# A 1x1 convolution to 128 channels as four tiles of 32 columns: one edit in a block-matching and convolution kernel

## The chip, the cores and the metric

The kernel runs on one core of a Trainium2 chip. The metric is the device time of one execution in microseconds (us). A core has five engines that run their own instruction streams in order and wait for each other by semaphores: TensorE (PE in the profile, with its weight loads under PEld), VectorE (DVE), ScalarE (ACT), GpSimd (POOL) and SyncE (SP). In this kernel the last two mostly issue DMAs.

## The reference

The input `x` is f32, 8 images of 32 channels of 128x128. Layer 0 normalises the image by groups of two channels and finds, for each pixel, the 8 of 25 shifts of the image whose 3x3 patches are nearest. It gathers the 8 shifted copies (32 x 8 = 256 channels), runs them through three pairs of a 1x1 convolution over all 256 channels and a 3x3 convolution of each channel by itself, and uses the result as a weight on a small transform of the gathered channels. Layer 1 is a 5x5 convolution of each channel. Cut to what matters:

```python
xb = _patch_match_stack(x)                                   # [8, 256, 128, 128]
dct = _conv(xb, dct_w, groups=C)
h = relu(_conv(_conv(xb, w1), w2, groups=CK, pad=1))         # w1, w3, w5: 256 x 256, 1x1
h = relu(_conv(_conv(h, w3), w4, groups=CK, pad=1))          # w2, w4, w6: 3x3 by channel
wiener = sigmoid(_conv(_conv(h, w5), w6, groups=CK, pad=1))
filt = _conv(wiener * dct, inv_dct_w, groups=C)
return _conv(filt, agg_w)
```

The change is in the 1x1 convolutions with w1, w3 and w5. All arithmetic in question is f32.

## The kernel before

An image is cut into 16 blocks of 8 rows (`R = 8`, `NS = 16`), with a 17th step that finishes the last rows. `steps` lists the 8 x 17 = 136 pairs of image and block. The main loop runs over the steps, and in each it works on four stages, `for i in (3, 2, 1, 0)`: the third, second and first pair of convolutions, each for a step that lies further back, and the end of layer 0. The instruction order of TensorE, VectorE and ScalarE is the order of the calls in this loop, written out by hand (`manual_schedule(engines=ORDERED)`). The order of the DMAs on POOL and SP is left to the scheduler.

The 256 channels are two halves of 128. Of each half a 1x1 convolution needs all 256 input channels, so two accumulating products (`g` in 0, 1) with 128 input channels each. The two halves of the output are treated differently:

- VectorE's half, output channels 128 to 255. `pointwise_v` (lines 639 to 657) computes the 1x1 convolution with channels on the partitions: for each tile of four rows (`h` in 0, 4) it takes a PSUM tile `ps` (named `pv...`) of 128 partitions x 512, and line 649 puts in the products of the weights `lhsT[:, g, P:CK]` (128 x 128) with four rows of 128 pixels. ScalarE copies the tile into `tv` (line 657). `depthwise_v` then does the 3x3 convolution: the first tap on ScalarE (line 700) and eight taps on VectorE (line 703), then the activation function (line 707).
- TensorE's half, output channels 0 to 127. `pointwise_t` (lines 659 to 687) writes 32 output channels and one of four rows into each quarter of the partitions, by products of 32 columns (line 673, tile `p...`), ScalarE copies them into `t` (line 680), and SP shifts rows between partitions by DMA (lines 685 and 687). `depthwise_t` does the 3x3 convolution by products of 32 columns with a banded matrix (line 729, tile `pw...`). ScalarE applies the activation (line 742).

Beside these, TensorE's stream holds the gather of the shifted copies (`gather_pixels`, line 611, tile `pg...`, 88 products of 32 columns at a time as the profile counts them), sums for the block matching (line 436, `pd`, 32 columns), the small transform and the end of layer 0 (line 788, `pc`, 64 columns; line 809, `pa`, 32 columns), transposes (lines 390, 502 and 546, 128 columns) and the 5x5 convolution of the image before (line 902, 64 columns).

Around a call of `pointwise_v` the order on TensorE is: `pointwise_v` of the stage; what other queues hold (`run("P")`, `final_dct`, `run("Q")`); `pointwise_t` of the same stage; `gather_pixels`; `depthwise_t` of the stage before. A product of f32 operands is two instructions with a weight load each in the profile, so a call of `pointwise_v` for a whole block (2 tiles x 2 halves) shows as 8 products.

The PSUM tiles of all these stages but `pw` and `pd` come from one pool, `ps_x`, with five buffers in turn.

Of the kernel before, what the change touches and what calls it, by code (L numbers as in the profile page):

```python
# [15 lines left out]
P = 128  # L16
C, K, H, W = 32, 8, 128, 128
CK = C * K
# [24 lines left out]
def bm3d_conv_preact(  # L43
# [16 lines left out]
    nc = tc.nc  # L60
# [578 lines left out]
    def pointwise_v(i, b, n, lhsT, src):  # L639

        v = tv[i - 1]
        if n == NS:
            nc.gpsimd.memset(v[:, i + 1 : 6], 0.0)
        r0, r1 = (i - 1 if n == 0 else 0), (R if n < NS else i - 1)
        for h in range(0, r1, 4):
            hr = min(4, r1 - h)
            ps = ps_x.tile([P, 4, W], F32, name=f"pv{i}_{b}_{n}_{h}", tag="x")
            for g in range(2):
                nc.tensor.matmul(  # L649
                    ps[:, :hr],  # L650
                    lhsT[:, g, P:CK],
                    src(g)[:, h : h + hr],
                    start=g == 0,
                    stop=g == 1,
                )
            a = max(h, r0)
            nc.scalar.copy(v[:, 2 + a : 2 + h + hr, 1 : 1 + W], ps[:, a - h : hr])  # L657

# [324 lines left out]
    def source(i, b, n):  # L983
        src = xbs.pop((b, n), None) if i == 1 else accs.pop((i - 1, b, n))
        return (lambda g: src[:, g]) if i == 1 else (lambda g: src[g])
# [27 lines left out]
    with tc.manual_schedule(engines=ORDERED):  # L1013
# [19 lines left out]
        for s in range(len(steps) + 2):  # L1033
# [10 lines left out]
            for i in (3, 2, 1, 0):  # L1044
# [6 lines left out]
                if live and i:  # L1051
                    src = source(i, bi, ni)
                    pointwise_v(i, bi, ni, lws[i - 1], src)
                    new_v, new_t = depthwise_v(i, bi, ni), depthwise_t(i, bi, ni)
                    accs[i, bi, ni] = [None, next(new_v)]
# [100 lines left out]
```

## Time and profile before

| | us |
|---|---|
| median of 3 runs | 6806.48 (6804.09 to 6808.73) |
| profiled execution, span | 6807.3 |
| TensorE busy, all | 6354.3 |
| of it products at line 649 (pv) | 980.7 + 477.4 |
| products at line 729 (pw) | 2144.1 |
| products at line 673 (p) | 989.1 + 468.1 |
| products at line 611 (pg) | 592.7 |
| VectorE busy, all | 5860.4 |
| of it line 703 (3x3 taps) | 4032.9 |
| ScalarE busy, all | 5064.6 |

The span is the time from the first to the last instruction of one profiled execution. Busy time is the time in which at least one instruction of an engine or group was under way; the products of a group overlap, so a busy time is less than the count times the mean. A form such as `128*32 128x512` is a product whose weights have 128 rows and 32 columns, with 512 streamed elements on each partition. The rows of the costliest groups that belong to the changed function and to its nearest kin (line, engine, operation, tiles, form, count, busy us, mean ns, idle before):

```profile
L673 PE MATMUL p<-acc,lw 128*32 128x256 f32 x16768 | 989.1, 381 | 25.3 <-ACT tv L657 22.7
L649 PE MATMUL pv<-acc,lw 128*128 128x512 f32 (+1 forms) x2112 | 980.7, 607 | 29.9 <-DVE acc L796 27.4
...
L657 ACT COPY tv<-pv 128x512 f32<-128x512 f32 (+2 forms) x784 | 438.1, 578 | 390.4 <-PE pv L649 374.2
```

Products into `p` and `pv` from `acc` handle as many channels and pixels: 16768 products of 32 columns and 256 elements are busy for 989.1 us, 2112 of 128 columns and 512 elements for 980.7 us. The same two stages have further groups that read `xb` in place of `acc`.

### The profile page before, as it was taken

How to read it: one execution, taken by the hardware profiler on the slowest of the kernel's cores; microseconds unless marked ns; L12 is line 12 of the kernel's file. 1: busy time of each engine (PE TensorE's matmuls, PEld its weight loads, DVE VectorE, ACT ScalarE, POOL GpSimd, SP SyncE). 2: the span in 40 equal slices, each digit the busy share in tenths (PEclk: the TensorE clock that was granted, in tenths of full speed). 3: DMA queues.
4: the chain of work that ended last, by engine and by line, in shares of the span. 5: the costliest groups of instructions: out<-in, count | busy, mean ns of one | idle time of the engine just before them, and what ended most of it. 6: DMA issues, size and time to landing. Idle time of an engine off the chain costs nothing.

```text
span 6807.3 us, 257036 instructions
## 1 busy us (share of the span) xinstructions
PE 6354.3 (93%) x113378; PEld 3352.8 (49%) x113378; DVE 5860.4 (86%) x8822; ACT 5064.6 (74%) x6698; POOL 3246.7 (48%) x5351
## 2 busy tenths in 40 slices
PE   5798899999999999999999999999999999999997
PEld 1454454554545455454554455545555454455553
DVE  7789988989889898898988888899888899877776
ACT  5787778777687777877777777877769777687772
POOL 7354446444464444544445444454436554344334
PEclk8899999999999999999999999999999999999998
DMA  4566656666566675666756656566665666566653
GB/s 90 143 153 153 151 149 154 159 152 158 147 156 155 144 169 135 163 151 152 167 135 158 161 146 169 138 165 159 149 150 151 162 156 152 138 170 157 154 151 80
DMA packets 809627, 1021.41 MB, mean 150 GB/s; under 512 B 255456, under 2 KB 619936, under 8 KB 808512
## 3 DMA queue, kind: packets, MB, share of 16 engines
q0 software_dynamic: 422432, 745.61, 42.9%
q1 hardware_dynamic: 383568, 258.11, 17.4%
q8 instruction: 892, 14.61, 0.9%
q10 hardware_dynamic: 2512, 1.25, 0.1%
q14 instruction: 223, 1.83, 0.1%
HBM read 553.25 MB, written 217.01 MB: 113 GB/s over the span
## 4 chain that ended last, share of the span: by engine, by line
PE 55%; DVE 23%; ACT 8%; DMA 6%; issue 5%; POOL 3%; SPq 0%; ACTq 0%; DVEq 0%; POOLq 0%
PE pw L729 18%; DVE acc L703 15%; PE pv L649 13%; PE p L673 12%; PE pg L611 4%; DVE df L421 3%; PE pc L788 2%; DMA t<-t 2%; PE p L902 2%; ACT df L429 2%; ACT ib L596 2%; DVE idx L514 1%; PE pa L809 1%; DMA xf<-xbd 1%; DVE acc L796 1%
## 5 line engine op out<-in xcount | busy, mean ns | idle before, releaser
L703 DVE SCALAR_TENSOR_TENSOR acc<-tv,dwv,acc 128x1024 f32<-128x1024 f32 (+3 forms) x3264 | 4032.9, 1237 | 249.6 <-ACT acc L700 140.3
L729 PE MATMUL pw<-t,dwd 96*32 96x254 f32 (+7 forms) x31680 | 2144.1, 422 | 84.7 <-issue 40.5
L729 PEld LDWEIGHTS pw<-t,dwd 96*32 96x32 f32 (+1 forms) x31680 | 1103.9, 111 | 906.6 <-issue 440.7
L582 POOL DMA_DIRECT2D ib<-idxd x1024 | 570.7, 558 | 1796.5 <-ACT sel L597 1620.6
L596 ACT ACTIVATE ib<-ib,nplace 128x1024 bf16<-128x1024 bf16 x1024 | 1170.1, 1143 | 9.5 <-DMA ib<-idxd 9.5
L597 ACT ACTIVATE sel<-ib 128x1024 f32<-128x1024 bf16 x1024 | 1084.8, 1059 | 32.5
L673 PE MATMUL p<-acc,lw 128*32 128x256 f32 x16768 | 989.1, 381 | 25.3 <-ACT tv L657 22.7
L649 PE MATMUL pv<-acc,lw 128*128 128x512 f32 (+1 forms) x2112 | 980.7, 607 | 29.9 <-DVE acc L796 27.4
L769 POOL DMA_DIRECT2D xf<-xbd x1088 | 650.2, 630 | 304.2 <-PE pc L788 87.0
L673 PEld LDWEIGHTS p<-acc,lw 128*32 128x32 f32 x16768 | 556.2, 111 | 454.9 <-ACT tv L657 62.5
L657 ACT COPY tv<-pv 128x512 f32<-128x512 f32 (+2 forms) x784 | 438.1, 578 | 390.4 <-PE pv L649 374.2
L611 PEld LDWEIGHTS pg<-sel,xt 128*32 128x32 f32 x45056 | 575.5, 111 | 252.1 <-issue 54.2
L429 ACT ACTIVATE df<-df 128x786 f32<-128x786 f32 (+2 forms) x576 | 468.0, 859 | 291.9 <-DVE df L421 289.2
L611 PE MATMUL pg<-sel,xt 128*32 128x48 f32 x45056 | 592.7, 207 | 80.4 <-ACT sel L597 46.0
L421 DVE TENSOR_TENSOR df<-xn 128x786 f32<-128x786 f32 (+2 forms) x576 | 532.5, 976 | 116.0 <-PE pd L436 109.2
L742 ACT ACTIVATE acc<-pw 128x512 f32<-128x512 f32 (+2 forms) x808 | 439.9, 573 | 249.7 <-PE pw L729 249.0
L649 PEld LDWEIGHTS pv<-acc,lw 128*128 128x128 f32 x2112 | 384.2, 193 | 475.6 <-issue 398.1
L707 ACT ACTIVATE acc<-acc 128x1024 f32<-128x1024 f32 (+3 forms) x408 | 416.8, 1022 | 229.7 <-DVE acc L703 229.5
L680 ACT COPY t<-p 128x512 f32<-128x512 f32 x800 | 424.6, 570 | 127.7 <-PE p L673 125.7
L700 ACT ACTIVATE acc<-tv,dwv 128x1024 f32<-128x1024 f32 (+3 forms) x408 | 454.5, 1114 | 52.6 <-PE pa L809 35.0
L649 PE MATMUL pv<-xb,lw 128*128 128x512 f32 x1024 | 477.4, 609 | 0.0
L673 PE MATMUL p<-xb,lw 128*32 128x256 f32 x8192 | 468.1, 380 | 4.4 <-DVE xy L914 4.4
(151 smaller groups left out, 5782.5 us busy)
## 6 DMA issues: line engine op xcount, KB each, us to landing
ib<-idxd POOLq DMA_DIRECT2D x1024, 256.0 KB, 4.4
xbd<-xb POOLq DMA_DIRECT2D x128, 1024.0 KB, 6.7
xf<-xbd POOLq DMA_DIRECT2D x960, 128.0 KB, 7.3
t<-t SPq DMA_DIRECT2D x792, 128.0 KB
t<-t SPq DMA_DIRECT2D x384, 256.0 KB
tv<-tv SPq DMA_DIRECT2D x384, 130.0 KB
xt<-xtd POOLq DMA_DIRECT2D x240, 176.0 KB, 4.6
xl<-xs POOLq DMA_DIRECT2D x256, 64.0 KB, 2.6
```

Of the source, the lines that this page charges most:

```text
L421: nc.vector.tensor_sub(df[:, :, ca:cz], xn[:, r0 : r0 + SR, ca:cz], xn[:, r0 + dy : r0 + dy + SR, ca + dx : cz + dx],)
L429: nc.scalar.activation(df[:, :, ca:cz], df[:, :, ca:cz], AF.Square)
L582: nc.gpsimd.dma_start(ib.rearrange("p k y x -> p (k y x)"), idxd[b][s4 // 8, s4 % 8, 4 * k0 : 4 * k0 + 8] .rearrange("k x -> (k x)") .part ...
L596: nc.scalar.activation(ib, ib, AF.Square, bias=nplace)
L597: nc.scalar.activation(sel, ib, AF.Relu, scale=-1.0, bias=1.0)
L611: nc.tensor.matmul(pg[C * j : C * (j + 1), :, xa:xz], xt[:, t], sels[j // 2][:, j % 2, :, xa:xz], start=True, stop=True,)
L649: nc.tensor.matmul(ps[:, :hr], lhsT[:, g, P:CK], src(g)[:, h : h + hr], start=g == 0, stop=g == 1,)
L673: nc.tensor.matmul(ps[C * r : C * (r + 1), e, :nb], lhsT[:, g, s], rows[:, r : r + 4 * nb - 3 : 4], start=g == 0, stop=g == 1,)
L700: nc.scalar.activation(acc, rows, AF.Copy, scale=tap)
L703: nc.vector.scalar_tensor_tensor(acc, rows, tap, acc, op0=ALU.mult, op1=ALU.add)
L729: nc.tensor.matmul(pt[u][C * j : C * (j + 1), ka:kz, :nb, xa:xz], dwd[0:hi, i - 1, u, j, dx + 1], t[0:hi, j, ka:kz, :nb, xa + dx : xz + dx ...
L769: nc.gpsimd.dma_start(xf[p : p + C, m, j0:j1], src[g, m, (h + m + 1) % 2, :, :, ya:yz])
```

## The change

In `pointwise_v` each product of 128 output columns becomes four products of 32 columns, `j` in 0 to 3. Product `j` takes the columns `P + 32 j` to `P + 32 (j + 1)` of the weights and writes the partitions `32 j` to `32 (j + 1)` of the same PSUM tile. All four stream the same rows. The loop over `g` stays outside, so each quarter still accumulates over the two halves of the input channels.

```diff
             for g in range(2):
-                nc.tensor.matmul(
-                    ps[:, :hr],
-                    lhsT[:, g, P:CK],
-                    src(g)[:, h : h + hr],
-                    start=g == 0,
-                    stop=g == 1,
-                )
+                for j in range(4):
+                    nc.tensor.matmul(
+                        ps[C * j : C * (j + 1), :hr],
+                        lhsT[:, g, P + C * j : P + C * (j + 1)],
+                        src(g)[:, h : h + hr],
+                        start=g == 0,
+                        stop=g == 1,
+                    )
             a = max(h, r0)
             nc.scalar.copy(v[:, 2 + a : 2 + h + hr, 1 : 1 + W], ps[:, a - h : hr])
```

The order of instructions on VectorE and ScalarE is the same in both programs, and so is that on TensorE apart from these products. Some DMA issues on POOL and SP stand in a slightly different order.

## The prediction

> **What bounds the kernel now.** I read the page's busy shares first, then the busy time by stretches, then the chain of waits, then the timeline of TensorE's weight loads, and last the list of TensorE's waits.
>
> ```profile
> PE 6354.3 (93%) x113378; PEld 3352.8 (49%) x113378; DVE 5860.4 (86%) x8822; ACT 5064.6 (74%) x6698; POOL 3246.7 (48%) x5351
> ...
> q8 instruction: 892, 14.61, 0.9%
> ...
> PE 55%; DVE 23%; ACT 8%; DMA 6%; issue 5%; POOL 3%; SPq 0%; ACTq 0%; DVEq 0%; POOLq 0%
> ```
>
> TensorE is busy for 93% of the span, VectorE for 86%. The chain that ended last runs over TensorE for 55% and over VectorE for 23%, so a saving on TensorE counts only in part. Busy time by stretches, first of everything, then of what touches pv, tells how much idle there is after the start-up (columns: microseconds, then busy time and instructions by engine, then granted clock, DMA share, GB/s):
>
> ```profile
> 270.00:6740.00 6470.00, 6178.01 (x111288) 3277.62 (x111287) 5632.97 (x8166) 4910.98 (x6484) 3044.41 (x5068) 0.98 0.62 152
> ...
> sum 6808.00, PE 1458.12 PEld 569.75 ACT 438.15; mean PE 486.04 PEld 189.92 ACT 146.05
> ```
>
> From 270 to 6740 us TensorE is idle for 6470.0 - 6178.0 = 292 us, 4.5%. The products into pv, which the change rewrites, keep it busy for 1458 us. The chain of the whole span gives L649 13.3%, 0.133 x 6807.3 = 905 us: 905 / 1458 = 62% of pv lies on the path that sets the end. A stretch of that chain, in order of time (start, length, what):
>
> ```profile
> 3023.29 0.80 PE pd L436 x8
> 3024.09 3.45 PE p L673 x64
> 3027.54 0.91 PE pg L611 x88
> 3028.45 3.63 PE pv L649 x8
> 3032.08 3.59 PE p L673 x64
> 3035.67 0.91 PE pg L611 x88
> 3036.59 5.17 PE pw L729 x96
> ```
>
> A pv stage (two tiles of four rows, two halves of the channels, two passes for each f32 product: 8 instructions) takes 3.63 us. The same 64 products into p take 3.45 us behind pd, which also works with 32 columns, and 3.59 us behind pv with its 128. Going from one width to the other has a price. The timeline of weight loads shows the pace within a stage, first of pv (128 columns), then of pw (four tiles of 32 columns, 508 or 512 streamed):
>
> ```profile
> 3028.38 0.30 PEld L649 LDWEIGHTS pv<-acc,lw 128*128 128x128 f32 x2
> 3028.92 0.19 PEld L649 LDWEIGHTS pv<-acc,lw 128*128 128x128 f32 x1 [0.24 <-issue]
> 3029.35 0.19 PEld L649 LDWEIGHTS pv<-acc,lw 128*128 128x128 f32 x1 [0.24 <-issue]
> ...
> 3003.39 0.16 PEld L729 LDWEIGHTS pw<-t,dwd 128*32 128x32 f32 x4 [0.27 <-issue]
> 3003.82 0.15 PEld L729 LDWEIGHTS pw<-t,dwd 128*32 128x32 f32 x4 [0.28 <-issue]
> 3004.25 0.16 PEld L729 LDWEIGHTS pw<-t,dwd 128*32 128x32 f32 x4 [0.27 <-issue]
> ```
>
> Both go at one round per 0.43 us: four 32-column products side by side last as long as one of 128 columns, and their four weight loads (0.16 us together) lie under the round.
>
> **The change, part by part.**
> *The products.* 3,136 pairs of load and product (x2112 and x1024 in the groups of L649) become 12,544: eight rounds of four in place of eight passes. The nearest rows are pw's 512-wide rounds. By the starts in the trace (medians), pv's eight starts span 3.108 us. Twelve pw rounds span 4.744 = 11 x 0.428 + 0.036, so eight rounds span 7 x 0.428 + 0.036 = 3.032: 0.076 saved. That is the first pass, 0.533 us against 0.429 for the others, becoming a plain round, less the stagger of the four.
> *The way in.* From the last start of pg to the first of pv 0.126 us pass, to the first of pw 0.012; from pw's last 256-wide round to pv 0.308, from p's last such round to pg, with no change of width, 0.196. So 0.112 to 0.114 goes.
> *The way out.* From pv's last start to a following p 0.522 us pass; with no change of width a 512-wide round would take 0.428 less its stagger of 0.020, 0.408. That is 0.114, and p's first round shrinks from 0.240 to 0.216, another 0.024. The sum, 0.138, is the 3.59 less 3.45 of the chain.
> *A whole stage.* 0.112 + 0.076 + 0.114 + 0.024 = 0.326 us. Counted in the trace, 305 of 400 runs of pv are followed by a product of 32 columns. Another 93 are followed by one of 128, where the switch only moves: out by 0.522 - 0.429 = 0.093 worse, in and within 0.188 better, 0.095 left. 305 x 0.326 + 93 x 0.095 = 108 us less on TensorE.
> *How much reaches the end.* By the chain 62%: 67 us. The bounds are all of it, 108, if TensorE alone sets the pace (it is idle for only 4.5%), and a quarter, 27, about half of TensorE's 55% of the chain, if VectorE's paths lead more often: where they lead, what TensorE saves becomes waiting.
> *The idle that grows.* 108 - 67 = 41 us turn into idle of TensorE. After 270 us the trace has 42 windows of half clock, 205 us long, 102 us of clock lost beside 292 us idle: 0.35 lost per us of idle. 41 x 0.35 = 14, of which 62% counts: 9 us given back.
> The Trainium skill, "TensorE: Matmul & The Clock Gate", Part 1, has the clock fall back only after an idle window of some 3.4 us; by that, idle in small pieces costs nothing and the time would be 9 us lower. The trace speaks against it in part: only 20 idle stretches exceed 3.4 us, and 42 windows are slow.
> *Instruction fetches.* 226,756 instructions of TensorE (113378 twice) over 892 packets of queue q8 are 254 each; 18,816 more are 74 more packets, 8.3%. What such a packet can cost stands among TensorE's waits for nothing that the profile shows:
>
> ```profile
> PE pw L729 <- issue: 40.5, 26, 4.2
> ...
> PE pg L611 <- issue: 28.3, 23, 3.6
> ...
> PE p L673 <- issue: 2.6, 2, 1.9
> ```
>
> In the trace 46 stops (63 us) lie whole multiples of 256 records apart. The three rows sum to 71.4 us, x 8.3% = 6 us more. It could be nothing, or double.
> *What costs nothing.* The copies tv<-pv read the same tile, wait for its last product and keep their length. VectorE's accumulation takes 1285 ns (median) under pv, pw and p alike, so four moving streams do not slow it. The orders on VectorE, ScalarE and, pv aside, TensorE are the same. SP keeps 1588 of 1621 places and POOL 5069 of 5356; nearly all others shift by one to three, and both queues have idle time (POOL is busy for 48%) that covers this.
> *Not in the trace:* four tiles that read the very same rows at once. Below, the gain of 0.326; above, the four loads no longer hidden, 8 x 0.16 - 0.33 = 0.95 us worse a stage, 400 x 0.95 x 0.62 = 236 us. I take the lower end, as pw is the same in all but that.
> *Sum* against this execution's span: 6807.3 - 67 + 9 + 6 = 6755 us. The runs' median, 6806.48, is 0.8 us from that span, so it is not converted.
>
> **The rivals.** *TensorE alone* (17%): all 108 us count and no idle is added, 6807.3 - 108 + 6 = 6705. For it: 4.5% idle; against: VectorE at 86% with 15% of the chain on L703.
> *VectorE takes over* (15%): a quarter counts, 6807.3 - 27 + 81 x 0.35 x 0.25 + 6 = 6793. For it: 38% of pv is off the chain already; against: VectorE is idle for 6470 - 5633 = 837 us after 270 us, three times TensorE's 292.
> *Nothing gained* (6%): 128 columns fill the array in one go, the pace per round stays, and each edge that I price is a matter of how starts are recorded rather than of time. Only the fetches remain: 6807.3 + 6 = 6813. Against: p's 3.45 and 3.59, measured end to end.
> The Trainium skill, "TensorEngine Tiling (Array Packing)", When to Use Tiling, names column tiles for stationary operands of at most 64 columns, which argues for this rival. Its Key Properties say that changing the tiling mode drains the engine, which argues for my forecast, and the 0.11 us edges agree.
> *Fetches decide* (8%), the slower side: pv was a rest for the fetches, 16 instructions in 3.6 us; now it has 64. A packet whose 254 instructions pass faster than the next one comes stops TensorE. The stops now sum to 71 us; when they pass 71 + 67 = 138 us the change loses. At three times, 6807.3 - 67 + 143 = 6883. Against: only 46 of 892 boundaries stop.
> *Not what it says* (2%): the four tiles run one behind the other or expose their loads, 6807 + 236 = 7043 or more. Against: p, pw and pg already run four abreast.
>
> **How the numbers follow.** The forecast, 6755, has 52%; its own range is 6733 (80% on the path) to 6784 (35%). From 6700 to 6800 the range takes in TensorE alone and VectorE's case; it leaves out the 16% of the last three rivals and a little below. About 0.2%, 13.6 us, can be told from no change. Faster: 52 + 17 + 10 of VectorE's 15 = 79%. Within 0.2%: 5 of VectorE's and 4 of nothing gained = 9%. Slower: 2 + 8 + 2 = 12%.
>
> **What would show it.** In the changed kernel: x12544 pairs of 128x32 into pv, loads in fours every 0.43 us; a chain piece of about 3.44 us for pv and 3.45 for p behind it; pv's 1458 us busy down by some 5%; TensorE's idle after 270 us up by about 40 us; q8 at about 966 packets and its stops below 90 us. I am wrong if rounds of pv come more than 0.43 + 0.33 / 8 = 0.47 us apart, if the p behind pv still takes 3.59, or if the stops at packet edges double.

## The result and the profile after

| | us |
|---|---|
| before, median of 6 runs | 6807.61 (6804.09 to 6817.41) |
| changed, median of 6 runs | 6784.58 (6756.88 to 6791.46) |
| ratio | 0.9949, 95% interval 0.9929 to 0.9968 |
| changed, profiled execution, span | 6789.7 |

The changed kernel is faster by 0.5%, 23 us by the medians. The forecast was 6755, 52 us below its span. Six further runs of the changed kernel gave 6772.88 beside 6809.58 before, a ratio of 0.9942 (0.9928 to 0.9957). All line numbers behind 649 are one higher in the changed kernel.

The page of the changed kernel, the lines that answer to those of before:

```profile
PE 6278.4 (92%) x122786; PEld 3307.5 (49%) x122786; DVE 5861.9 (86%) x8822; ACT 5061.5 (75%) x6698; POOL 3246.9 (48%) x5351
...
q8 instruction: 965, 15.81, 1.0%
...
PE 53%; DVE 24%; ACT 8%; DMA 6%; issue 6%; POOL 2%; SPq 0%; ACTq 0%; DVEq 0%; POOLq 0%
...
L650 PE MATMUL pv<-acc,lw 128*32 128x512 f32 x8448 | 965.8, 593 | 43.1 <-DVE acc L797 32.3
...
L650 PE MATMUL pv<-xb,lw 128*32 128x512 f32 x4096 | 475.7, 596 | 0.0
```

TensorE has 9,408 more products, all of them in pv (8448 + 4096 = 12,544 for 3,136), and is busy for 75.9 us less. "Issue" has gone from 5% to 6% of the chain. The chain of waits in a stretch like that of before (start, length, what):

```profile
3005.30 0.80 PE pd L436 x8
3006.09 3.45 PE p L674 x64
3009.55 0.91 PE pg L611 x88
3010.46 3.44 PE pv L650 x32
3013.89 3.45 PE p L674 x64
3017.35 0.91 PE pg L611 x88
3018.26 5.16 PE pw L730 x96
```

The pv stage takes 3.44 us where it took 3.63, and the p stage behind it 3.45 where it took 3.59, now the same as the p behind pd. Here the edit does all that was expected. The weight loads in the timeline of the same pv stage:

```profile
3011.13 0.14 PEld L650 LDWEIGHTS pv<-acc,lw 128*32 128x32 f32 x4 [0.29 <-issue]
3011.56 0.14 PEld L650 LDWEIGHTS pv<-acc,lw 128*32 128x32 f32 x4 [0.29 <-issue]
3011.99 0.14 PEld L650 LDWEIGHTS pv<-acc,lw 128*32 128x32 f32 x4 [0.29 <-issue]
```

Four loads at a time, 0.43 us apart: four tiles that stream the very same rows keep the pace of pw. Some 40 us later the same chain shows what takes the gain back:

```profile
3051.75 3.45 PE p L674 x64
3055.20 0.76 PE pg L611 x71
3055.96 2.50 issue
3058.46 0.36 PE pg L611 x17
```

In the middle of a gather of 88 products TensorE stands for 2.50 us, waiting for no other engine. TensorE's waits over the span have such stops in the rows with issue; the row with DMA is the wait for the rows that SP shifts (us in total, times, longest):

```profile
PE pg L611 <- issue: 45.8, 28, 4.7
...
PE pw L730 <- DMA t<-t: 41.3, 23, 4.1
PE pw L730 <- issue: 40.2, 29, 4.2
...
PE pv L650 <- issue: 8.2, 5, 3.4
...
PE p L674 <- issue: 2.5, 2, 2.1
```

The four rows with issue sum to 96.7 us, where before it was 71.4. Busy time by stretches, first of all, then of pv alone:

```profile
270.00:6740.00 6470.00, 6112.39 (x120617) 3233.19 (x120612) 5641.38 (x8193) 4907.66 (x6488) 3055.75 (x5085) 0.98 0.63 153
...
sum 6790.00, PE 1441.43 PEld 446.83 ACT 437.97; mean PE 480.48 PEld 148.94 ACT 145.99
```

TensorE is idle for 6470.0 - 6112.4 = 358 us in this stretch, 66 more than before.

Since TensorE works through one queue, its time is work at full clock, idle, and clock lost in half-clock windows. Two profiles of each kernel were taken (the second ones are among the experiments). Counted in their traces from 270 to 6740 us, with a stop at a packet edge being an idle piece over 0.15 us at a record that lies a whole multiple of 256 from the others and that the profile puts down to issue:

| us | before | changed | difference of the means |
|---|---|---|---|
| span | 6807.3, 6792.7 | 6789.7, 6774.8 | -17.8 |
| stops at packet edges | 62.6, 68.6 | 95.2, 97.4 | +30.7 |
| other idle | 226.1, 229.9 | 259.5, 244.5 | +24.0 |
| clock lost (half of the half-clock windows) | 102.4, 92.2 | 139.9, 138.2 | +41.8 |
| work at the edges of the pv stages, as predicted | | | -108 |

The last four sum to -11.5, 6 us from the measured -17.8.

Two of these rows are rough: half of a half-clock window counts clock as lost also where TensorE stood idle in it, and the last row is the predicted one. The traces give both directly. TensorE's busy time from 270 us to the end, less half of its busy time in half-clock windows, is its work at full clock: 6117.2 and 6119.0 us before, 6013.4 and 6016.4 changed. That is 103 us of work saved, where 108 were predicted. The clock lost over busy time alone is 88.7 and 70.1 before, 116.2 and 112.5 changed, 35 more. Idle pieces over 0.15 us, to the end as well, are 50 us more. So -103 + 35 + 50 = -18, as it has to be where the three fill the span.

Of the other idle one part grows in both profiles: the wait of pw for the shifted rows, 41.3 and 44.7 us changed, where it was 27.5 and 30.3. That is 14 of the 24 us. Its row before:

```profile
PE pw L729 <- DMA t<-t: 27.5, 19, 4.4
```

The edges, by medians of starts in the first profile of the changed kernel: 0.012 from pg into pv (predicted 0.012), 3.028 within (3.032), 0.409 out to p or pa (0.408), and 0.523 out to a 128-column transpose (0.522).

### The profile page after: what moved, and what is told of

Same layout as the page of the kernel before. It is cut to its first block, busy times and chain, and to the rows that moved or that the text cites. A ratio compares the mean times of both kernels' runs of the same rounds, so it can differ in the third digit from the quotient of the medians.

```text
span 6789.7 us, 275809 instructions
## 1 busy us (share of the span) xinstructions
PE 6278.4 (92%) x122786; PEld 3307.5 (49%) x122786; DVE 5861.9 (86%) x8822; ACT 5061.5 (75%) x6698; POOL 3246.9 (48%) x5351
## 4 chain that ended last, share of the span: by engine, by line
PE 53%; DVE 24%; ACT 8%; DMA 6%; issue 6%; POOL 2%; SPq 0%; ACTq 0%; DVEq 0%; POOLq 0%
PE pw L730 18%; DVE acc L704 16%; PE pv L650 13%; PE p L674 12%; PE pg L611 4%; DMA t<-t 3%; DVE df L421 3%; PE pc L789 2%; ACT ib L596 2%; PE p L903 2%; ACT df L429 2%; DVE idx L514 1%; PE pd L436 1%; ACT acc L701 1%; PE pa L810 1%
## 5 line engine op out<-in xcount | busy, mean ns | idle before, releaser
L704 DVE SCALAR_TENSOR_TENSOR acc<-tv,dwv,acc 128x1024 f32<-128x1024 f32 (+3 forms) x3264 | 4033.0, 1237 | 256.8 <-ACT acc L701 150.1
L730 PE MATMUL pw<-t,dwd 96*32 96x254 f32 (+7 forms) x31680 | 2164.3, 424 | 98.1 <-DMA t<-t 41.3
L730 PEld LDWEIGHTS pw<-t,dwd 96*32 96x32 f32 (+1 forms) x31680 | 1121.3, 111 | 918.3 <-issue 443.7
L650 PE MATMUL pv<-acc,lw 128*32 128x512 f32 x8448 | 965.8, 593 | 43.1 <-DVE acc L797 32.3
L674 PEld LDWEIGHTS p<-acc,lw 128*32 128x32 f32 x16768 | 586.9, 111 | 430.1 <-issue 78.1
L611 PEld LDWEIGHTS pg<-sel,xt 128*32 128x32 f32 x45056 | 586.7, 111 | 267.2 <-issue 70.1
L658 ACT COPY tv<-pv 128x512 f32<-128x512 f32 (+2 forms) x784 | 438.0, 578 | 351.3 <-PE pv L650 340.4
L650 PEld LDWEIGHTS pv<-acc,lw 128*32 128x32 f32 x8448 | 283.7, 111 | 533.4 <-issue 436.5
L650 PE MATMUL pv<-xb,lw 128*32 128x512 f32 x4096 | 475.7, 596 | 0.0
```

The costliest lines, as they stand in the source:

```text
L611: nc.tensor.matmul(pg[C * j : C * (j + 1), :, xa:xz], xt[:, t], sels[j // 2][:, j % 2, :, xa:xz], start=True, stop=True,)
L650: nc.tensor.matmul(ps[C * j : C * (j + 1), :hr], lhsT[:, g, P + C * j : P + C * (j + 1)], src(g)[:, h : h + hr], start=g == 0, stop=g == 1,)
L674: nc.tensor.matmul(ps[C * r : C * (r + 1), e, :nb], lhsT[:, g, s], rows[:, r : r + 4 * nb - 3 : 4], start=g == 0, stop=g == 1,)
L704: nc.vector.scalar_tensor_tensor(acc, rows, tap, acc, op0=ALU.mult, op1=ALU.add)
L730: nc.tensor.matmul(pt[u][C * j : C * (j + 1), ka:kz, :nb, xa:xz], dwd[0:hi, i - 1, u, j, dx + 1], t[0:hi, j, ka:kz, :nb, xa + dx : xz + dx ...
```

## The experiments

Every run but the second profile of before was timed in rounds beside runs of the kernel before on the same chip.

**The changed kernel once more**, no edit.

> The changed kernel once more, for a second profile and more times: its six times so far lie at 6757 (two) and at 6783 to 6791 (four). Theory (saved 108 us at the edges of the pv stages, given back as instruction-fetch stops, 63 to 95 us, and as half-clock windows, 205 to 280 us): a median near 6785, and a quicker execution would show fewer stops or fewer half-clock windows, with pv's rounds unchanged. Rival (the six times are noise about one value): times spread evenly from 6755 to 6795 with stops and windows alike in both profiles.

Measured: 6772.88 (6755.63 to 6776.6) beside 6809.58. The profiled execution, 15 us shorter than the first, has 97.4 us of stops (71 of them) and 138.2 us of lost clock, as many as the first, and 15 us less of other idle. So the theory was wrong that a quicker execution shows fewer stops or windows. Both are steady, as the rival had them, and the difference of these two executions lies in the other idle.

**The kernel before once more**, no edit.

> The kernel before once more, for a second profile. If the stops and half-clock windows of one profile are typical, it shows 55 to 75 us of stops at packet edges and 180 to 220 us of half-clock windows; if chance rules them, as much as the changed kernel's 95 and 280 us can appear here too.

Measured: one time, 6794.44, with 68.6 us of stops and 184.3 us of half-clock windows (before: 62.6 and 204.8). Both profiles of before lie well under both of the changed kernel in stops and in lost clock: the differences in the table are larger than those between two profiles of one kernel, though two of each is few.

**Two products of 64 columns.** Is it the narrow products, or the change of width around them?

```diff
-                for j in range(4):
+                for j in range(2):
                     nc.tensor.matmul(
-                        ps[C * j : C * (j + 1), :hr],
-                        lhsT[:, g, P + C * j : P + C * (j + 1)],
+                        ps[64 * j : 64 * (j + 1), :hr],
+                        lhsT[:, g, P + 64 * j : P + 64 * (j + 1)],
...
```

> Two products of 64 columns in place of four of 32. Theory (the gain is the change of width at the way in and out, 0.11 us each, which 64 columns beside 32 still pay): no gain, and 6,272 more instructions to fetch, so 6805 to 6825; the way out of pv stays at 0.52 us and the p stage behind it keeps its longer first round. Rival (narrow products side by side are quicker in themselves): about half of the gain or more, 6785 to 6797.

Measured: 6816.45, ratio 1.0013 (1.0002 to 1.0023): no gain. Its chain of waits:

```profile
3072.27 3.45 PE p L674 x64
...
3078.45 3.58 PE pv L650 x16
3082.03 3.59 PE p L674 x64
```

The p behind pv has its 3.59 us again, and by the starts in the trace the way in is 0.126 us and the way out 0.523, as with 128 columns. The stage is 0.05 us shorter, 3.58 for 3.63, all of it within the stage (3.062 us from the first start to the last, where it was 3.108), but a way out to a 128-column transpose now takes 0.523 too, where it took 0.429. TensorE's work at full clock, counted as above, is 6116.7 us, as before. So what the edit to 32 columns saves is the change of width: 64 beside 32 columns pays it like 128 beside 32. The 24 packets more (916) hardly change the stops, some 67 us, and the wait of pw for the DMA is 39.3 us here too, without a gain in pv: why that wait grows is not shown.

**Each stream of 512 as two of 256**, in the changed kernel: the same work, twice the instructions in pv.

```diff
-            for g in range(2):
-                for j in range(4):
+            for q in range(0, hr, 2):
+                z = min(q + 2, hr)
+                for g in range(2):
+                    for j in range(4):
...
-                        ps[C * j : C * (j + 1), :hr],
+                            ps[C * j : C * (j + 1), q:z],
...
-                        src(g)[:, h : h + hr],
+                            src(g)[:, h + q : h + z],
...
```

> The changed kernel with each 512-wide stream as two of 256: the same widths of weights, 25,088 more instructions of TensorE, some 99 more fetch packets (965 to 1064). Work on TensorE grows by about 8 x 4 ns a stage, 13 us in all. Theory (fetches give back part of the gain): stops at packet edges grow from 95 to 140 us or more and the time to 6815 to 6840, no better than before the change. Rival (the extra stops were chance): stops stay near 95 us and the time near 6792.

Measured: 6825.36, ratio 1.0023 (1.001 to 1.0035): the whole gain is gone. The page and the list of TensorE's waits:

```profile
q8 instruction: 1061, 17.38, 1.1%
```

```profile
PE pg L611 <- issue: 50.0, 39, 3.6
...
PE pw L732 <- issue: 43.7, 32, 3.8
...
PE pv L652 <- issue: 31.1, 22, 4.7
...
PE p L676 <- issue: 7.7, 8, 1.7
```

96 packets more bring the stops at their edges to 137.7 us, 41 more than in the changed kernel, and pv itself is now hit (31.1 us, where it was 8.2). With 8 us of added work at the edges of the rounds (3.458 us of starts a stage against 3.437, 384 times) that would be 49, near the 52 us by which the time rose over the changed kernel in the same rounds (6825.36 against 6772.88). But the nearness is chance. The ledger of this run has 209.4 us of other idle and 117.8 of lost clock, 43 and 21 less than the changed kernel's two profiles, so the stops in part took the place of other waits; and the work at full clock is 6043.6 us, 29 more than in the changed kernel, where the edges of the rounds give 8. That more instructions for the same products cost the whole gain is shown. That a stop costs what it lasts is not, and what the other 21 us of work are made of stays open.

**More instructions in the kernel before**, pv untouched: the second stage's pw products of 512 as pairs of 256.

```diff
-                    for j in range(4 if kz > ka else 0):
-                        nc.tensor.matmul(
-                            pt[u][C * j : C * (j + 1), ka:kz, :nb, xa:xz],
+                    for k in range(ka, kz):
+                        for j in range(4):
+                            nc.tensor.matmul(
+                                pt[u][C * j : C * (j + 1), k : k + 1, :nb, xa:xz],
...
```

> The kernel before, pv untouched, with the 512-wide products of the second stage's pw as pairs of 256: 12,288 more instructions, some 48 more packets (892 to 940), no change of any width; its rounds grow by 128 x 12 x 4 ns, 6 us. Theory (fetch stops scale with instructions): stops from 63 to about 84 us, time 6818 to 6835. Rival: stops near 63 us, time 6808 to 6813.

Measured: 6818.07, ratio 1.0014 (1.0002 to 1.0026). Packets 941, stops 91.3 us, some 26 more than in the two profiles of before. The time rose by 8.5 us only: the other idle fell to 200.2 (228 before) as the stops grew. So here a stop in part replaces a wait that would have come anyway. The stops grew as the theory had it, or a little more; the time came out at the low end of its range.

**VectorE relieved.** Four of the eight taps on VectorE are left out of each 3x3 convolution of its half, in the kernel before and in the changed one.

```diff
-            ((1, 1), (0, 0), (0, 1), (0, 2), (1, 0), (1, 2), (2, 0), (2, 1), (2, 2))
+            ((1, 1), (0, 0), (0, 1), (0, 2), (1, 0))
```

> The kernel before with four of VectorE's eight taps left out of each 3x3 convolution of its half (some 2000 us less on VectorE). It is only the base for the next run. TensorE's work is unchanged, so if TensorE leads for most of the span the time falls only by part of its idle, to 6600 to 6750; if VectorE led in most places it falls further.

> The changed kernel with the same four taps left out, to be set against the run before it. Theory (38% of the 108 us saved went into waits for VectorE's chains): with VectorE relieved the difference grows from 23 to 37 us as measured so far to 60 to 100 us, and less idle comes back. Rival (the loss is fetch stops and half-clock windows alone, VectorE has no part): the difference stays at 20 to 45 us and the stops grow by some 33 us again.

Measured: 6550.16 (6538.2 to 6551.54) and 6490.29 (6483.84 to 6523.93), a difference of 60 us, where the full kernels have 23 and 37. The first lies below the 6600 to 6750 that were expected if TensorE leads, so by that reading VectorE led in more places of the full kernel. The pages, first without and then with the change:

```profile
PE 6263.1 (96%) x113378; PEld 3301.0 (50%) x113378; DVE 3869.8 (59%) x7190; ACT 5073.7 (78%) x6698; POOL 3251.3 (50%) x5351
```

```profile
PE 6178.9 (95%) x122786; PEld 3277.4 (51%) x122786; DVE 3872.5 (60%) x7190; ACT 5067.4 (78%) x6698; POOL 3251.4 (50%) x5351
```

With VectorE at 60% busy the change brings twice as much, at the lower end of what the theory had. The ledger of this pair, from 270 us to the end: stops 61.7 to 73.8 (+12), other idle 72.1 to 80.3 (+8), lost clock 46.4 to 70.6 (+24), with -108 a sum of -64, beside spans that differ by 58. The work at full clock falls by 102 us, as in the full kernels. All three repayments shrink: the other idle from +24 to +8, and the stops and the lost clock by 18 us each, which neither theory foresaw. So VectorE's load has a part in the loss, but not as plain waits for VectorE alone: 9 of the 16 us by which the other idle shrinks are again pw's wait for the DMA t<-t (12.9 us in the first of this pair, 17.9 in the second, so +5 where it was +14). Even with VectorE far from busy the change does not give its 108 us.

**Fewer instructions in the changed kernel.** If fetches cost that much, pw's split into two parts of 256 should go. First in both stages that have it, then in one.

```diff
-        parts = ((1, 2), (0, 1)) if i != 2 and n < NS else ((0, 2),)
+        parts = ((0, 2),)
```

> The changed kernel with pw's products of the first and third stage no longer split into two parts of 256: some 24,600 instructions of TensorE fewer, about 868 packets instead of 965. Theory (fetch stops cost what they last): stops fall from 95 us to 50 or less and the time by up to 45 us, to 6735 to 6760, if the rows that the DMA shifts are there in time. Rival (the split hides the wait for the shifted rows): waits of pw for the DMA t<-t grow from 41 us by more than the stops fall, time 6780 to 6850.

Measured: 6822.99, ratio to before 1.0031 (1.0019 to 1.0043). Packets fell to 869 and the stops to 30.1 us, 66 less. The first line of TensorE's waits has the price:

```profile
PE pw L730 <- DMA t<-t: 125.3, 52, 6.6
```

The wait for the rows that SP shifts rose by 84 us, from 41.3. The rival was right.

The split kept in one stage (`i == 1` or `i == 3` in place of `i != 2`):

> The changed kernel with pw split into two parts of 256 only in the first stage (the third in one part of 512): 12,288 instructions of TensorE fewer, about 917 packets. Theory (a fetch stop costs what it lasts, and the third stage has pv and p of the second between the DMA and its pw, as the second has of the first): stops from 95 to about 65 us, waits of pw for the DMA t<-t no higher than 60 us, time 6745 to 6770, the quickest so far. Rival (the third stage needs its split): the DMA waits grow by 40 us or more and the time is 6790 to 6815.

> The changed kernel with pw split only in the third stage (the first in one part): the same 12,288 instructions fewer. Theory (the first stage's pw runs in the part of the loop that has no pv and p, so its DMA is hidden least): stops near 65 us, DMA waits of pw at 90 us or more, time 6790 to 6820. Rival: as quick as the run before it or quicker.

Measured: 6798.27, ratio 0.9982 (0.9969 to 0.9994), with the split in the first stage, where 6745 to 6770 was expected, and 6834.21, 1.0036 (1.0023 to 1.0048), with it in the third, where 6790 to 6820 was. Stops fell to 67.9 and 62.3 us, the waits for the DMA rose to 93.7 and 108.1. The first stage needs its split more, as expected, but the theory that the third can do without was wrong: against the changed kernel both lose. No kernel tried here that computes the whole result beats the changed one.

## Why the prediction was right, and where its sizes were off

The direction, the range of 6700 to 6800 and the mechanism held; the gain was 23 to 37 us where 52 was forecast. That the range held is in part luck: two terms were too small by 58 us together (stops 31 for 6, lost clock 42 for 9), and 17 us of that was covered because the step before them withheld 41 us as waits of which the traces show 24.

- *The products, the way in, the way out:* right to 0.01 us each, and shown to be the change of width by the run with 64 columns. TensorE's work fell by 103 us for 108. Four tiles on the same rows, which no trace had, took the lower end as chosen.
- *What costs nothing:* VectorE's accumulation is busy for 4033.0 us after and 4032.9 before, the copies tv<-pv for 438.0 and 438.1. This held. That the slack of the DMA queues covers their small shifts is not shown: pw's wait for the rows that SP shifts grew by 14 us, for a reason that stays open.
- *Instruction fetches, 6 us:* mis-sized, they took 31. The step scaled the stops by the number of instructions (8.3%). They grow faster: +47% in time for 8% more packets, +110% for 19% more (137.7 over 65.6). The stops of 95.2 and 97.4 us also passed the 90 named as the sign. The rival "fetches decide" had it that pv was a rest of 16 instructions in 3.6 us in which the next packet could arrive. That is not shown: 48 packets more in pw, with pv untouched, brought some 26 us of stops too. The rival's size was off as well; with 25,088 further instructions the stops reach 137.7 us, and the gain is gone.
- *The idle that grows, 9 us of clock:* mis-sized, the lost clock rose by 42 (35 where counted over busy time alone). The step took idle times a rate of 0.35 and then 62% of it; idle rose by 55 (30.7 + 24.0), and every lost microsecond counts on TensorE. Even 55 x 0.35 = 19 is less than half of 42. The last section has what lies behind it.
- *How much reaches the end, 62%:* the wrong form for this term. The share of the chain was applied to the saving alone, as if the rest turned to plain waits of 41 us. The traces show 24 us of other idle, and 14 of them are the wait for SP's rows, not for VectorE; the rest of the loss is in the two terms above, which a chain of the kernel before cannot show, since they answer to the new stream of instructions.
- *The two rules that were weighed:* the rule that a change of tiling mode drains the engine (the Trainium skill, "TensorEngine Tiling (Array Packing)", Key Properties) agrees with the 0.11 us an edge here; that this time is a drain, no run shows. The one in When to Use Tiling of the same page, column tiles for at most 64 columns, would have kept 128: here the four tiles pay because their neighbours are tiled.
- *Busy time of pv* was to fall by some 5% and fell by 1.1% (1458.1 to 1441.4). The busy time is a union of spans that overlap the neighbours' and contains the slow windows; it was the wrong row for such an edge.

## What to carry to other kernels

Where TensorE alternates between narrow and wide products, price each change of width at both ends, and consider giving the wide ones the neighbours' width even if nothing is gained inside. Price the added instructions too, and not in proportion: here 8% more packets of instructions brought 47% more time in stops. A saving on a busy engine is best followed by its own ledger of work, idle by cause, and lost clock.

## What the runs showed of the hardware that was not expected

*Instruction fetch can stop TensorE.* A packet of queue q8 holds 256 instructions of TensorE (226,756 loads and products and the 1,633 of its sequencer in the trace before, over 892), and the stops lie whole multiples of 256 such records apart. Stops at packet edges took 62.6 us with 892 packets, 95.2 with 965, 137.7 with 1061 and 30.1 with 869, but some 67 with 916, each kernel with its own order of dense and sparse stages.

*The clock falls on little more than half a window of idle, in pieces.* The trace's clock changes on a grid of 3.41 us. In how many windows of that grid at full clock, from 270 to 6400 us, TensorE was idle for how long in sum, and how often a half-clock window followed:

| idle in a window of 3.41 us | before: windows, followed by half clock | changed |
|---|---|---|
| under 1.2 us | 1644, 0 | 1604, 0 |
| 1.2 to 1.7 us | 44, 1 | 51, 3 |
| 1.7 to 2.3 us | 31, 21 | 45, 32 |
| over 2.3 us | 18, 18 | 19, 19 |

In all twelve traces of this case together, every window with more than 2.05 us of idle was followed by half clock (379 of 379), 115 of 266 between 1.65 and 2.05, 18 of 506 between 1.2 and 1.65, and none of 19,646 under 1.2. So some 2 us of idle is enough, little more than half of a window and not a whole one. Pieces add up: three windows before with 2.2 to 2.4 us in sum, none of them in a single stretch over 1.6, were followed by half clock too. Short waits cost nothing in clock up to there, and up to some 1.7 us (half of 3.41) beyond it, a window at a time. The changed kernel has more windows past 1.7 us, 64 against 49. "TensorE: Matmul & The Clock Gate", Part 1, in the Trainium skill asks for an idle window; these traces show that little more than its half suffices. That more stops at fetches push more windows over the edge is likely but not shown: the run with the most stops (137.7 us) lost 117.8 us of clock, less than the changed kernel's 139. What decides which waits fall together stays open.
